# A Mamba/attention block with a mixture of experts on one core: narrower wide tiles, one sigmoid pass, and work moved among the stages

## The chip, the cores and the metric

The kernel runs on one core of a Trainium2 chip. It is one program of 28297 profiled instructions. The time is the device time of one execution in microseconds (us); "before" is the median of three timed executions. A separate execution was taken by the hardware profiler; all rows below come from it.

The engines run beside each other, each in the order in which its instructions were written out: PE (matrix products into PSUM[...]), DVE (vector work), ACT (activation functions, with a table that has to be loaded for some of them), POOL (vector work and scatters), and SP, which issues most DMAs. An instruction that waits holds up everything behind it on its engine.

## What is computed

All arithmetic is f32. The input x is 4 images of 256 channels by 32 x 32 positions (1024 positions per image). Cut to what matters here:

```
xn = norm(x) per position
for each of 4 channel groups: mamba           # project u and z, causal conv, SiLU, dt, a scan over
                                              # 1024 positions with 16 states x 128 channels
g  = sigmoid(conv(conv(x_concat)))            # the gates
xg = g * xm
R  = conv1x1(conv3(xg)) + xg
xm2 = conv1x1(conv3(concat(xs, R))) + xs      # the first half of conv3 is of the image itself: "own taps"
x_local = conv3(xm2);  x_global = attention(xm2), 8 heads
x_out = gelu(norm(concat(x_local, x_global) @ fc))
image = proj(norm(depthwise 3x3(norm(x_out)))) + x
# mixture of experts on the 4096 positions ("rows")
top 2 of 8 experts by gate logits, softmax weights
out = rows + sum over both experts of w * (gelu(row @ W1 + b1) @ W2 + b2)     # 256 -> 1024 -> 256
```

## The kernel before, in words

**The order is written out by hand.** Inside `tc.manual_schedule` (L1482) each engine executes in the order in which the Python code emits. The emission is a loop of ticks: `beat()` (L1441) advances every running generator, and each generator says with `yield n` in how many ticks it wants to go on. `start` adds generators, `one_by_one` chains them, `behind_flag` holds one back until a flag is set. `in_turn` (L411) makes items (usually products into PSUM) and uses each `lag` ticks later, one item every `every` ticks.

**The scan sets the ticks.** For each image, 4 channel groups n and 2 halves h are "parts"; a part has 16 steps (`scan`, L789). Each step emits on ACT the decay of three steps later (`decay`, `LEAD = 3`), on DVE one product into PSUM (`inflow`, L684) and one scan (`step`, L695), and on POOL one product (L703). `before`, `behind` and `group` (L739 to L755) say at which step of a part the preparations for the next one are emitted; `group[0]` holds the projections of z and u of the next channel group, the copies of z from PSUM, and SiLU, which loads its table, works on u and z, and loads back the table for Exp and Ln.

**Images overlap.** While image b is scanned, image b-1 goes through `convolutions` (parts 0 to 2), then `attention` in a pause of the scan after part 3, then `joined` (output projection and `fc`, norm, Gelu), in parts 4 and on. Image b-2 goes through `around` (3x3 taps) in the pause and `sent_off` (norm, projection, `experts.dispatch`) beside `joined`. `dispatch` finds for each row its place among the rows of its expert and scatters the rows to `XS` in DRAM, by 16 scatters on POOL per image. At the end of the scan, image 3 still has to go through all of this and image 2 through `around` and `sent_off`; the expert tiles are emitted between their pieces. A variable `pace` says every how many ticks a piece of a tile comes.

**Gates.** In `convolutions`, four products `gp` (two channel halves c, two position halves) are made; `sigmoid` reads them out of PSUM with ACT's Sigmoid, which needs its own table, and then loads the table for Exp and Ln again. This happens once for each c. POOL multiplies with the gates, then come ACT and DVE for the three taps. The generator `side` makes the products `fx` of the image's own taps and is advanced at every second tick of `gating`.

**Own taps.** For image 2 the own taps are computed earlier, in `normalised`, and kept in DRAM (`XD`); for the other images `convolutions` computes them first thing (`depthwise3` with `fdw_w`: one ACT and two DVE operations for each c).

**Expert tiles.** A tile is 256 rows of one expert. The tiles come in four series: two of 8 tiles that are full after images 1 and 2, the "rest" (19) and the "wide" ones (8) after image 3. A wide tile has 384 rows, so that an expert whose last tile would hold at most 128 rows needs none for them. Sixteen tiles of the first two series run, then 4 groups of one wide and 3 rest tiles. The last 7 rest tiles and the last 4 wide ones (`LATE`, `LATE_WIDE`) stand in a branch at the end and run only if a table has that many entries. For tile n+1, `ahead` emits during tile n the load of its rows (once the image's rows are sent), the load of its weights (2 MB), and `front` (transposes on PE, a copy to `xT` on DVE, four small DVE operations). `tile` then makes the hidden layer (`h`, L2174), Gelu on ACT, the second layer (`y`, L2186) by blocks of 128 rows, bias and weight on DVE, and one scatter with addition per block on POOL.

Of the kernel before, what the change touches and what calls it, by code (L numbers as in the profile page):

```python
# [9 lines left out]
F32 = mybir.dt.float32  # L10
# [38 lines left out]
LATE, LATE_WIDE = 7, 4  # L49
# [23 lines left out]
def network(  # L73
# [41 lines left out]
    XD = {b: dram.tile([P, NC2, N], F32, name=f"XD_{b}") for b in (2,) if b < B}  # L115
# [29 lines left out]
    with tc.tile_pool(name="w_conv", bufs=1) as wp, tc.tile_pool(  # L145
# [345 lines left out]
        def normalised(b):  # L491
# [30 lines left out]
            for c in range(NC2):  # L522
# [11 lines left out]
                if b in XD:  # L534
                    xd = a4(f"taps_{b}_{c}")
                    nc.scalar.activation(
                        xd, xl, AF.Identity, bias=col("fdw_b", c), scale=col("fdw_w", 3 * c + 1)
                    )
                    yield 1
                    for k, to, at in (  # L540
                        (0, slice(1, N), slice(0, N - 1)), (2, slice(0, N - 1), slice(1, N)),
                    ):
                        nc.vector.scalar_tensor_tensor(
                            xd[:, to], xl[:, at], col("fdw_w", 3 * c + k), xd[:, to],
                            ALU.mult, ALU.add,
                        )
                        yield 1
                    nc.sync.dma_start(XD[b][:, c, :], xd)

# [182 lines left out]
        def add_skip(b, n, h):  # L732
            c, rows = where(n)
            if n == 0 and h == 0:
# [16 lines left out]
                2: [(stack_x, 0)], 3: [(project_z, 0), (stack_x, 1)], 5: [(copy_z, 0)], 6: [(project_z, 1)],  # L751
                7: [(project_u, 0)], 8: [(copy_z, 1), (project_u, 1)], 12: [(silu,)],
# [94 lines left out]
        def convolutions(b):  # L847
# [41 lines left out]
            gs = []  # L889

            def sigmoid(c, gp):
                gs.append(a4(f"g_{b}_{c}"))
                for h in range(2):
                    nc.scalar.activation(  # L894
                        gs[c][:, half(h)], gp[h], AF.Sigmoid, bias=col("qpw_b", c)
                    )
                loaded[0] = None
                log_exp()

            def gating():  # L900
                yield from in_turn(range(NC2), gate, sigmoid)
# [29 lines left out]
            for n, ticks in enumerate(gating()):  # L931
                if n % 2 == 0:
                    next(side, None)
                yield ticks
# [20 lines left out]
            for _ in range(4):  # L955
# [197 lines left out]
        def inverse_deviation(name, xc, alone):  # L1153
# [9 lines left out]
            if alone:  # L1163
# [8 lines left out]
                yield 1  # L1172
            else:
# [12 lines left out]
        def joined(b):  # L1186
# [12 lines left out]
                ), every=2 if b == 0 else 1,  # L1199
            )  # L1200

            xc = XC[b] = a8(f"xc_{b}")
# [1136 lines left out]
```

## Time and profile before

| | us |
|---|---|
| timed executions: median (lowest to highest of 3) | 2253.38 (2250.92 to 2259.66) |
| the profiled execution's own time | 2258.26 |
| its span, first to last instruction | 2256.8 |
| busy in the span: PE, DVE, ACT, POOL | 1994.9, 1539.5, 1234.5, 1046.1 |
| scan's last step ends | about 1486 |
| attention of image 3 | about 1660 to 1746 |
| PE's last product of a tile | 2218.5 |

A row of a group reads: line, engine, operation, output<-inputs, shapes, count; then busy us and mean ns of one; then the idle time of the engine just before these instructions and what ended most of it. A row of a timeline reads: start, length, engine, line, operation, shapes, count and, in brackets, idle time before it and who ended it. A row of waits reads: who waited for whom, us in total, how many times, the longest. An f32 product shows as two records on PE. In the 40 slices of the page, PE is near full through the last third:

```
PE   6877878999978999987979999669999999999995
DVE  3989999768998978788898977984355265111111
```

### The profile page before, as it was taken

The page shows a single profiled execution, that of the slowest core. Times are in us where ns is not written, and L with a number is a line of the kernel's source. Part 1 is how long each engine was busy: PE and PEld are TensorE (multiplying, and loading weights), DVE is VectorE, ACT ScalarE, POOL GpSimd, SP SyncE. Part 2 cuts the span into 40 slices and gives each one's busy share as a digit, 9 for nine tenths or more (in the row PEclk, how much of TensorE's full clock was granted, in tenths as well). Part 3 has the DMA queues.
Part 4 walks back from the last instruction along what each step waited for, and adds up shares of the span by engine and source line. Part 5 has one row for each costly group of instructions (what it writes and reads, how often), then busy time and mean ns, then how long its engine had stood idle before and what let it go on. Part 6 is the DMA issues. An engine that isn't in the chain of part 4 may idle for free. (4 is left out here: it accounts for less than half of the span.)

```text
span 2256.8 us, 28297 instructions
## 1 busy us (share of the span) xinstructions
PE 1994.9 (88%) x8766; PEld 895.8 (40%) x8766; DVE 1539.5 (68%) x2211; ACT 1234.5 (55%) x2297; POOL 1046.1 (46%) x930
## 2 busy tenths in 40 slices
PE   6877878999978999987979999669999999999995
PEld 2112112322212332322223234125742677888884
DVE  3989999768998978788898977984355265111111
ACT  4665666678767676775756777325358422222221
POOL 0788878613877730675985035742040021422221
PEclk8898999999999999998899999779999999999997
DMA  3555553401453421243544013343240175866655
GB/s 99 140 155 125 123 136 76 118 10 56 119 131 86 99 48 38 71 113 84 157 98 100 20 37 91 80 154 95 92 118 1 45 216 164 257 186 180 168 160 161
DMA packets 156816, 248.79 MB, mean 110 GB/s; under 512 B 34597, under 2 KB 101701, under 8 KB 156521
## 3 DMA queue, kind: packets, MB, share of 16 engines
q1 hardware_dynamic: 136032, 220.59, 35.8%
q0 software_dynamic: 12976, 17.58, 4.0%
q10 hardware_dynamic: 7640, 8.65, 1.2%
q8 instruction: 73, 1.20, 0.2%
q14 instruction: 95, 0.77, 0.1%
HBM read 135.39 MB, written 35.84 MB: 76 GB/s over the span
## 5 line engine op out<-in xcount | busy, mean ns | idle before, releaser
L703 POOL TENSOR_TENSOR dA<-hs,cs 128x512 f32<-128x512 f32 x512 | 682.0, 1340 | 414.9 <-DVE hs L695 279.7
L674 ACT ACTIVATE dA<-dts,A 128x512 f32<-128x512 f32 x512 | 359.2, 718 | 190.8 <-DMA dts<-dt 105.7
L2206 POOL DMA_INDIRECT Y<-ys,dest x68 | 109.7, 1613 | 532.5 <-DVE ys L2200 525.7
L713 PE MATMUL yp<-dA,quads 128*32 128x512 f32 x1024 | 277.7, 638 | 71.9 <-POOL dA L703 60.9
L2179 ACT ACTIVATE hs<-h,b 128x256 f32<-128x256 f32 (+1 forms) x256 | 112.2, 485 | 384.2 <-PE h L2174 279.1
L1078 ACT ACTIVATE e<-st 128x512 f32<-128x512 f32 x512 | 264.0, 603 | 102.0 <-PE st L1068 84.3
L684 DVE TENSOR_TENSOR dBu<-dts,bs 128x512 f32<-128x512 f32 x384 | 260.3, 679 | 82.3 <-ACT g L894 14.0
L2174 PE MATMUL h<-xT,w 128*128 128x256 f32 (+1 forms) x1024 | 247.7, 398 | 13.5 <-DVE xT L2146 13.5
L2186 PE MATMUL y<-w,hs 128*128 128x256 f32 x1088 | 250.2, 382 | 5.0 <-ACT hs L2179 5.0
L695 DVE TENSOR_TENSOR_SCAN hs<-dA,last,dBu 128x512 f32<-128x512 f32 x192 | 243.9, 1270 | 3.5 <-POOL dt L624 1.7
L695 DVE TENSOR_TENSOR_SCAN hs<-dA,dBu 128x512 f32<-128x512 f32 x192 | 232.1, 1209 | 11.6 <-PE av L1088 3.9
L1124 DVE TENSOR_TENSOR e<-e,e 128x512 f32<-128x512 f32 x256 | 170.0, 727 | 83.8 <-ACT e L1078 45.8
L2174 PEld LDWEIGHTS h<-xT,w 128*128 128x128 f32 x1024 | 196.8, 193 | 64.8 <-DVE xT L2146 15.2
L2186 PEld LDWEIGHTS y<-w,hs 128*128 128x128 f32 x1088 | 205.8, 192 | 39.0 <-issue 6.1
L666 PE MATMUL bs<-u,xpwT_s 128*32 128x512 f32 x1024 | 161.3, 661 | 61.4 <-DVE hs L695 32.6
L2146 DVE COPY xT<-xp 128x512 f32<-128x512 f32 (+1 forms) x36 | 23.4, 660 | 268.1 <-PE xp L2143 242.7
L1068 PE MATMUL st<-qk 32*128 32x512 f32 x1024 | 175.9, 641 | 4.3 <-DVE ys L2195 2.7
L713 PEld LDWEIGHTS yp<-dA,quads 128*32 128x32 f32 x1024 | 49.8, 113 | 278.5 <-POOL dA L703 175.3
L1114 PE MATMUL av<-e,v 128*32 128x512 f32 x1024 | 139.9, 609 | 0.0
L1068 PEld LDWEIGHTS st<-qk 32*128 32x128 f32 x1024 | 60.0, 184 | 120.4 <-issue 87.5
L1088 PE MATMUL av<-e,every 128*32 128x512 f32 x512 | 87.7, 601 | 3.8 <-DVE e L1124 3.8
L666 PEld LDWEIGHTS bs<-u,xpwT_s 128*32 128x32 f32 x1024 | 25.1, 112 | 158.2 <-issue 58.1
(324 smaller groups left out, 2773.0 us busy)
## 6 DMA issues: line engine op xcount, KB each, us to landing
dts<-dt SPq DMA_DIRECT2D x512, 128.0 KB
w<-in_W_dram SPq DMA_DIRECT2D x124, 512.0 KB
cs<-cd SPq DMA_DIRECT2D x512, 64.0 KB
xd<-xn SPq DMA_DIRECT2D x64, 128.0 KB
xs<-XS SPq DMA_DIRECT2D x28, 260.0 KB
xn<-in_x_dram SPq DMA_DIRECT2D x8, 512.0 KB
XL<-xl SPq DMA_DIRECT2D x8, 512.0 KB
xl<-XL SPq DMA_DIRECT2D x4, 1024.0 KB
```

Source lines behind the costliest of these rows:

```text
L666: nc.tensor.matmul(bs[r], xpwT_s[:, n, s : s + 1].to_broadcast([P, 32]), T[b, n, "u"][:, half(h)], start=True, stop=True,)
L674: nc.scalar.activation(dA, T[b, n, h, "dts", g][:, 0, :], AF.Exp, scale=A[:, g, n, q : q + 1])
L684: nc.vector.tensor_tensor(dBu, T[b, n, h, "dts", g][:, 1, :], T[b, n, h, "bs", q], ALU.mult)
L695: nc.vector.tensor_tensor_scan(hs, T[b, n, h, "dA", i], dBu, 0.0 if h == 0 else last, ALU.mult, ALU.add)
L703: nc.gpsimd.tensor_tensor(dA, hs, T[b, n, h, "cs", q], ALU.mult)
L713: nc.tensor.matmul(T[b, n, h, "yp"][ts(g, 32)], quads, T[b, n, h, "dA", q * GD + g], start=False, stop=(q == GS - 1),)
L1068: nc.tensor.matmul(sts[i], k[r, ts(kt, P)], q[r, half(h)], start=True, stop=not shifted)
L1078: nc.scalar.activation(es[i], sts[i], AF.Exp, scale=1.0 / HD**0.5)
L1114: nc.tensor.matmul(accs[0][ts(i, HD)], v8[:, kt, ts(4 * g + i, HD)], es[i], start=(kt == 0), stop=(kt == NK - 1),)
L1124: nc.vector.tensor_tensor(first[i], first[i], es[i], ALU.add)
L2174: nc.tensor.matmul(hp[:, i, :], w1(c, k0 + i), xT[:, c, :], start=(c == 0), stop=(c == NC2 - 1))
L2186: nc.tensor.matmul(yp[:, ts(t % 2, C)], hidden(k)[:, ts(t, P)], w2(k), start=(k == 0), stop=(k == NHC - 1),)
```

## The change

- **Wide tiles of 320 rows** instead of 384 (`REST = 64`). Their third block has 64 rows. Its rows are loaded by a DMA of their own, its small DVE operations run apart, its second layer puts the products of even and odd k into the two halves of PSUM's partitions (`parts`), and ACT and DVE add the halves. The rest series has 21 entries, 9 of them late; 12 still run in the main stretch.
- **Gates**: `keep` copies `gp` out of PSUM with Identity and the bias; after the second c both are passed through Sigmoid in SBUF. For the last image the table for Exp and Ln isn't loaded right after, nor after the Gelu of its `joined`.
- **`side`** starts four ticks later and ends in the residual products.
- **Image 3's own taps** are computed by `taps_ahead` in the last pause, behind `local` and `around`, from `XL` into `XD`, and `convolutions` loads them.
- **`group[0]`**: second projection of z at step 4 (was 6), its copy at 7 (8), the projections of u at 8 and 10 (7 and 8), SiLU at 13 (12).
- **`joined` of image 2**: an item every second tick in both products, and `fc` waits until image 1's projection is emitted. **`inverse_deviation` of image 1** interleaves its two halves (8 ticks instead of 11).
- **`dispatch` of image 2** scatters at every second tick (each tick before).
- **`tiles`**: while a tile isn't ready, the generator looks again after 1 or 2 ticks instead of 4.

```diff
-LATE, LATE_WIDE = 7, 4
+LATE, LATE_WIDE = 9, 4
+REST = 64
...
-    XD = {b: dram.tile([P, NC2, N], F32, name=f"XD_{b}") for b in (2,) if b < B}
+    XD = {b: dram.tile([P, NC2, N], F32, name=f"XD_{b}") for b in (2, 3) if b < B}
...
+                if b in XD and b < B - 1:
+                    yield from own_taps(b, c, xl)
...
+        def taps_ahead(b):
+            for c in range(NC2):
+                xl = a4(f"xt_{b}_{c}")
+                nc.sync.dma_start(xl, XL[b][:, c, :])
+                yield 2
+                yield from own_taps(b, c, xl)
...
-                2: [(stack_x, 0)], 3: [(project_z, 0), (stack_x, 1)], 5: [(copy_z, 0)], 6: [(project_z, 1)],
-                7: [(project_u, 0)], 8: [(copy_z, 1), (project_u, 1)], 12: [(silu,)],
+                2: [(stack_x, 0)], 3: [(project_z, 0), (stack_x, 1)], 4: [(project_z, 1)],
+                5: [(copy_z, 0)], 7: [(copy_z, 1)], 8: [(project_u, 0)], 10: [(project_u, 1)], 13: [(silu,)],
...
-            def sigmoid(c, gp):
-                gs.append(a4(f"g_{b}_{c}"))
+            gs = [a4(f"g_{b}_{c}") for c in range(NC2)]
+            def keep(c, gp):
                 for h in range(2):
                     nc.scalar.activation(
-                        gs[c][:, half(h)], gp[h], AF.Sigmoid, bias=col("qpw_b", c)
+                        gs[c][:, half(h)], gp[h], AF.Identity, bias=col("qpw_b", c)
                     )
-                loaded[0] = None
-                log_exp()
+                if c == NC2 - 1:
+                    for g in gs:
+                        nc.scalar.activation(g, g, AF.Sigmoid)
+                    loaded[0] = None
+                    if beside:
+                        log_exp()
...
             for n, ticks in enumerate(gating()):
-                if n % 2 == 0:
+                if n >= 4 and n % 2 == 0:
                     next(side, None)
...
-            for _ in range(4):
+            for n in range(4):
+                if n % 2 == 0:
+                    next(side, None)
                 yield next(gated)
...
+            elif quick:
+                sq, var = [], []
+                for at in range(6):
+                    if at < 2:
+                        sq.append(squares(at))
+                    if 2 <= at < 4:
+                        var.append(column_mean(f"var_{name}_{at - 2}", sq[at - 2]))
+                    if 4 <= at:
+                        root(r[:, half(at - 4)], var[at - 4], eps5)
+                    yield 1
...
-                ), every=2 if b == 0 else 1,
+                ), every=2 if b in (0, B - 2) else 1,
             )
+            while b == B - 2 and not T.get(("projected", b - 1)):
+                yield 1
...
-                ), lag=(4, 4, 2, 2)[b], every=(4, 2, 1, 1)[b],
+                ), lag=(4, 4, 2, 2)[b], every=(4, 2, 2, 1)[b],
...
-            log_exp()
+            if b < B - 1:
+                log_exp()
...
-                    yield 4
+                    yield 2 if n in xs else 1 if n in got else 4
...
+                                *([taps_ahead(b)] if b == B - 1 and b in XD else []),
...
-    SERIES = (8, 8, 19, 8)
+    SERIES = (8, 8, 21, 8)
...
-                yield 2 if b == 0 or b == 1 and t % 2 else 1
+                yield 2 if b in (0, 2) or b == 1 and t % 2 else 1
...
-        return self.T + P if s == self.WIDE else self.T
+        return self.T + REST if s == self.WIDE else self.T
...
+            parts = P // n
             for k in range(NHC):
                 nc.tensor.matmul(
-                    yp[:, ts(t % 2, C)], hidden(k)[:, ts(t, P)], w2(k),
-                    start=(k == 0), stop=(k == NHC - 1),
+                    yp[ts(k % parts, n), ts(t % 2, C)], hidden(k)[:, ds(t * P, n)], w2(k),
+                    start=(k < parts), stop=(k >= NHC - parts),
                 )
...
+            if parts > 1:
+                other = m0.tile([REST, C], F32, tag="other", name=f"other_{j}", bufs=1)
+                nc.scalar.copy(other, yp[n:P, 0:C])
+                nc.vector.tensor_tensor(other, other, b2_s[0:n], ALU.add)
+                nc.vector.tensor_tensor(ys[0:n, t], yp[0:n, 0:C], other, ALU.add)
```

## The prediction

> **What bounds the kernel now.** I read the stretches first (busy microseconds by engine in each window), because the kernel has parts with different limits.
>
> ```profile
> core 0: us, PE busy (x) PEld busy (x) DVE busy (x) ACT busy (x) POOL busy (x), PEclk, DMA share, GB/s
> 55.50:300.60 245.10, 192.40 (x668) 44.78 (x668) 234.66 (x271) 148.58 (x281) 200.74 (x165) 0.91 0.56 136
> ...
> 1200.00:1318.00 118.00, 116.58 (x710) 33.61 (x710) 95.97 (x126) 85.51 (x165) 21.92 (x19) 1.00 0.16 42
> 1318.00:1486.00 168.00, 135.36 (x466) 43.62 (x465) 147.09 (x215) 90.75 (x172) 106.50 (x102) 0.87 0.35 95
> 1486.00:1660.00 174.00, 150.56 (x596) 100.66 (x596) 79.01 (x160) 63.01 (x99) 35.85 (x45) 0.95 0.38 112
> ...
> 1919.00:2218.50 299.50, 299.08 (x1362) 251.10 (x1362) 51.66 (x165) 68.85 (x152) 81.88 (x89) 1.00 0.65 179
> ```
>
> Until 1486 us the state scan runs and DVE sets the pace: 235 of 245 us busy in the first full stretch, a step being one scan and one product, about 1.7 us. The three attention pauses in it (1200:1318 is the last) are PE's. From 1486 on PE does the rest, and from 1919 to 2218 it is never idle, so there only PE work counts. Of the 174 us after the scan PE works 151. The waits of PE there, in total and longest:
>
> ```profile
> PE h L2174 <- DVE xT L2146: 10.5, 1, 10.5
> PE y L2186 <- ACT hs L2179: 4.4, 1, 4.4
> PE xp L2143 <- DMA xs<-XS: 1.5, 1, 1.5
> PE gp L884 <- ACT qs L877: 1.5, 1, 1.5
> ...
> PE op L730 <- POOL xl L365: 1.0, 1, 1.0
> ```
>
> These 19 us lie between 1490 and 1533, and PE is the bound from there until the last tile: each one filled with tile work ends the kernel so much earlier. After PE's last matmul of a tile (2218.5) come 38 us of adding rows, reading back and writing out, which nothing here touches.
>
> **Part by part.**
>
> *Tiles of 320 rows.* The rows of PE for one wide tile (start, length; a row ends in effect where the next starts):
>
> ```profile
> 1962.44 10.48 PE L2174 MATMUL h<-xT,w 128*128 128x384 f32 x32
> 1972.76 3.62 PE L2186 MATMUL y<-w,hs 128*128 128x256 f32 x16
> ...
> 1976.65 7.07 PE L2186 MATMUL y<-w,hs 128*128 128x256 f32 x32
> 1983.56 7.07 PE L2174 MATMUL h<-xT,w 128*128 128x256 f32 x32
> ```
>
> The first layer takes 10.32 us for 32 records of 384 columns (322 ns each); the next tile takes 6.91 for 32 of 256 (216). So 64 columns are worth 53 ns, and 320 columns save 32 x 53 = 1.7 us. The third block's second layer is 16 records of 216 ns, 3.45 us. With 64 rows it has as many records, but the even and the odd ones go to different halves of the array's columns. Whether halves overlap I read from the row that already uses column groups, four of them:
>
> ```profile
> 1497.04 2.78 PE L870 MATMUL qd<-xm,qdwT_s 128*32 128x512 f32 x24
> ```
>
> 24 records of 512 columns one after another would take 24 x 0.43 = 10.3 us; they take 2.78, four at a time. So I let two at a time take half: 1.7 us saved. Against it speaks the Trainium skill, "TensorEngine Tiling (Array Packing)", Key Properties: changing the tiling mode drains the engine, and this block changes it twice in each tile. The trace has the price:
>
> ```profile
> 1367.87 1.02 PE L608 MATMUL dtp<-u,wdt 128*128 128x512 f32 x2
> 1368.82 1.06 PE L666 MATMUL bs<-u,xpwT_s 128*32 128x512 f32 x8
> 1369.70 1.04 PE L713 MATMUL yp<-dA,quads 128*32 128x512 f32 x8
> 1370.70 1.55 PE L406 MATMUL var_lgn<-sq_lgn,ones_mean 128*128 128x512 f32 x3
> ```
>
> Two full records need 0.86 and the narrow ones start after 0.95; eight narrow ones need 0.86 and the full ones start after 1.00. A change costs about 0.1, so the rule takes 0.2 back per tile. The half-size transposes give 0.2 (6 records took 0.66). Sum 3.4 per tile, **13.8 us** for four. Were the halves served in turn, it would be about 7; that is the lower end. The added ACT copy and two DVE additions (0.6 and up to 0.7 each by the rows of like size), the split row load and the four extra small DVE operations are covered by ACT and DVE that are busy 69 and 52 of 299 us; uncovered they would cost 2 us per tile. Running the reference's routing on its inputs gives 1024, 1065, 1023, 1012, 1006, 1048, 1041, 973 rows per expert: three exceed a multiple of 256 by 1 to 64, so the same 32 tiles run, four wide, and no late one.
>
> *After the scan.* Image 3's own taps (2 ACT operations of 1.24, 4 DVE of 1.28 us) leave the head of the stretch; tile 0's front is asked for every tick or second tick instead of every fourth; the sigmoids cost one table load, not two pairs. Today tile 0's xT copy stands on DVE at 1509.6 behind four of those taps (5.1 us) and ten of `around`'s (11.6 us), though its rows landed at 1495. Image 1's last rows are sent three ticks earlier by the quick variance (some 5 us), so xT should be there by about 1492. PE gets 10 us of tile work for the 10.5 us hole. The 4.4 us hole is ACT's:
>
> ```profile
> 1522.58 1.28 ACT L894 ACT_TABLE_LOAD   x1
> 1523.88 1.27 ACT L894 ACTIVATE g<-gp,V 128x512 f32<-128x512 f32 x2
> 1525.16 1.28 ACT L381 ACT_TABLE_LOAD   x1
> 1526.45 1.28 ACT L894 ACT_TABLE_LOAD   x1
> ...
> 1530.32 1.28 ACT L2179 ACT_TABLE_LOAD   x1
> ```
>
> Nine microseconds until the tile's next Gelu become 4 copies (2.5), two sigmoids (2.1) and 2 loads (2.6), the copies apart from the rest: 4.7 in one piece. I count 15 of the 19 us; what remains is the landing of the rows and the wait of `op`. Ends: 6 (image 3's chain is late for its products and PE waits there) and 19. What is late next is PE itself. **15 us**.
>
> *Image 2's row scatters at every second tick.* 16 scatters go through POOL and its queue in front of attention; at its start DVE's ys addition is late and PE waits 2.7 us (page: st, 4.3 idle, 2.7 by ys). Attention has over 30 ticks for 32, POOL is idle there (12 of 86 us), and their first reader is tile 8, after it. **2 us**, ends 0 and 2.7.
>
> *Image 2's join slowed, image 1's variance quick.* After the third pause two images' chains issue products at once. DVE's waits there:
>
> ```profile
> DVE hs L695 <- issue: 3.5, 1, 3.5
> DVE dBu L684 <- PE bs L666: 3.1, 1, 3.1
> DVE dBu L684 <- ACT xm L736: 2.6, 1, 2.6
> DVE dBu L684 <- ACT xglo L1197: 2.3, 2, 1.7
> ```
>
> With three smaller ones (1.1, 1.0, 1.0) they make 14.6 us. Half the products per tick and the second chain waiting for the first removes what PE's crowding causes; the Gelu and its loads (5 us of ACT) come later in the scan and may cost a step. I take two thirds, **10 us**, ends 0 and 14.6. The wait for image 1's projection ends some 18 ticks in, the join some 40, of 64: nothing after the scan waits for it.
>
> *Gates beside the scan (three images).* DVE waits 14.0 us in six places for ACT's g, which holds PSUM banks through a table load. The copies free them; fx products leave the crowded ticks. But ACT's block does not shrink much: 7.7 us become 2.4 + 1.28 + 2.1 + 1.28 = 7.1, now 4.7 in one piece, and SiLU (1.28 + 1.27 + 1.05 + 1.28 = 4.9) comes a step nearer. `decay` is three steps, 5.1 us, ahead. Here the Trainium skill, "ScalarE: Activation LUTs", What ACT_TABLE_LOAD costs, differs: 2.66 us per switch with its drain; the rows show 1.28 and the next activation 0.01 to 0.02 later. By the page two switches fewer save 5.3 us of ACT per image, by the row 2.6, which the two extra passes (2.1) nearly use up. I go by the row: **5 us** of the 14, ends -3 and 13.
>
> *z, u and SiLU moved.* DVE waited 4.6 us in all for z; SiLU one step later leaves three steps to `project_dt`. Zero, ends -5 and +4.6.
>
> *Image 3's taps in the pause.* DVE works 96 of 118 us there, PE bounds it; 5.1 us of DVE, 2.5 of ACT, two loads and two stores on SP's queue (DMA share 0.16) fit, the last tap perhaps after it. SP's stores wait for DVE, and the first spread loads behind them are ten steps away. Zero; uncovered 5.
>
> Sum: 13.8 + 15 + 2 + 10 + 5 = 45.8 us. The profiled execution took 2258.26 us (span 2256.8 and 1.5 around it), 4.9 above the median 2253.38. From it 2212.5; from the median **2208 us**.
>
> **Rivals.** (1) *The scan gives nothing*: the freed waits come back as ACT waits of the decays, since ACT's work there is nearly unchanged. For it: the 4.7 and 4.9 us blocks against 5.1 us of lead; against: the PE waits of the join are not ACT's. 30.8 saved, 2223. (2) *The hole moves*: PE starts tile 0 early, then waits for image 3's gates; 5 of 15 saved, 2218. Against it: some 20 us of tile pieces precede the first products. (3) *Halves in turn*: 2214. (4) *Everything goes*: join 14.6, gates 13: 2195. (5) *Slower, by late tiles*: one expert too many with a small rest, or over 12 tiles left, and the closing branch runs all 13 late tiles, 9 x 14.3 + 4 x 17.3 = 198 us, 2406. It decides with the first tile over; by the row counts four wide places and twelve others are exactly filled, and one row moved to the next expert changes neither. (6) *No change*.
>
> **How the numbers follow.** Forecast 0.38; (1) 0.22, (2) 0.14, (3) 0.08, (4) 0.12, (5) 0.02, (6) 0.03, 0.01 for another loss. The forecast's own terms vary by about 9 us either way (2199 to 2217); (1) with (2) reaches 2230, (4) with a bit more 2191: the range is 2191 to 2230. A measurement tells 0.5% (11 us) from no change; all but the last three cases are faster by more: 0.94, 0.03, 0.03.
>
> **What would show it.** The h row of a wide tile at 8.6 us, its third block at about 1.75 for 16 records; no PE wait for xT over 3 us after the scan; PE from the scan's end to attention some 15 us shorter; the stretch after the third pause some 10 us shorter; four loads at the sigmoid line instead of eight. Wrong if DVE's waits on dA grow where those on g fall, if PE waits for rp's or gp's inputs between 1490 and 1550, or if a late tile appears.

## The result, and the profile after

The changed kernel takes 2218.06 us (median of 6, 2211.61 to 2225.49) against 2254.15 us for the kernel before (median of 6). The ratio is 0.9839, with an interval of 0.9819 to 0.9858. So 36 us are saved where 45.8 were forecast. In a later comparison it took 2213.3 us against 2253.12, ratio 0.9841 (0.9816 to 0.9866). The direction and the range held, and the forecast itself was 10 us too low (5 against the second measurement).

The profiled execution of the changed kernel took 2211.61 us, the shortest of its six. That of the kernel before took 2258.26, above the median. Between the spans of the two profiles (2256.8 and 2209.9) lie 46.9 us, almost the sum of the forecast. The difference between 46.9 and 36 needs an explanation of its own, which is given below.

Busy microseconds by engine in stretches of the changed kernel's scan (the first full image, the third pause, the rest):

```profile
core 0: us, PE busy (x) PEld busy (x) DVE busy (x) ACT busy (x) POOL busy (x), PEclk, DMA share, GB/s
56.10:298.10 242.00, 193.76 (x668) 44.64 (x668) 234.16 (x272) 148.97 (x281) 200.35 (x165) 0.90 0.57 139
1181.00:1297.00 116.00, 113.81 (x694) 32.73 (x690) 95.85 (x125) 83.32 (x159) 18.64 (x15) 1.00 0.16 40
1296.10:1464.30 168.20, 135.53 (x465) 41.21 (x464) 145.98 (x215) 92.34 (x175) 108.41 (x105) 0.88 0.38 104
```

The picture of limits is the old one: DVE paces the scan, PE the rest. The scan ends at 1464.3 instead of 1485.1, which is 20.8 us earlier. From there to PE's last product of a tile it is one PE-bound stretch. I compare it with the same stretch of the kernel before, first before, then after:

```profile
1485.10:2218.30 733.20, 701.25 (x3269) 501.75 (x3268) 263.21 (x640) 260.08 (x497) 160.81 (x186) 0.98 0.48 136
```

```profile
1464.30:2170.40 706.10, 683.52 (x3269) 490.67 (x3270) 262.27 (x656) 257.74 (x500) 159.85 (x182) 0.99 0.50 143
```

The stretch is 27.1 us shorter: PE is busy for 17.7 us less (701.25 to 683.52), and its holes shrink by 9.4 us (31.95 to 22.58, each as stretch less busy time). The end after the last product stayed within 1 us of its 38.5.

The same stretch in four stages (up to attention, attention, from there to the 14th tile, and from the 14th tile to the last), first before, then after:

```profile
1485.20:1655.50 170.30, 148.92 (x587) 99.98 (x586) 79.22 (x160) 62.46 (x97) 34.70 (x44) 0.95 0.37 109
1655.50:1747.30 91.80, 89.11 (x641) 25.09 (x640) 51.40 (x79) 69.63 (x137) 14.15 (x20) 0.98 0.12 34
1747.30:1919.30 172.00, 164.19 (x685) 125.62 (x684) 81.26 (x238) 59.15 (x111) 29.98 (x34) 0.97 0.49 141
1919.30:2218.30 299.00, 298.94 (x1362) 251.06 (x1362) 51.23 (x164) 68.85 (x152) 81.88 (x89) 1.00 0.65 179
```

```profile
1464.30:1625.00 160.70, 148.56 (x588) 101.24 (x592) 73.46 (x148) 57.74 (x94) 25.39 (x24) 0.94 0.40 122
1625.00:1711.00 86.00, 86.00 (x640) 24.29 (x632) 53.27 (x89) 69.51 (x137) 23.13 (x35) 1.00 0.15 45
1711.00:1881.70 170.70, 160.26 (x686) 122.10 (x685) 81.05 (x238) 61.86 (x113) 30.93 (x36) 1.00 0.50 143
1881.70:2170.50 288.80, 288.80 (x1362) 243.10 (x1362) 54.50 (x184) 68.63 (x156) 80.39 (x87) 1.00 0.67 184
```

From first product to first product, the stages became shorter by 10.0, 5.4, 1.4 and 10.2 us.

The rows of PE around one wide tile (start, length, shapes, count):

```profile
1920.66 1.16 PE L2194 MATMUL xp<-ident,xs 128*128 128x128 f32 x6
1921.74 3.72 PE L2248 MATMUL y<-w,hs 128*128 128x256 f32 x16
1925.30 8.78 PE L2235 MATMUL h<-xT,w 128*128 128x320 f32 x32
1933.92 3.62 PE L2248 MATMUL y<-w,hs 128*128 128x256 f32 x16
...
1937.81 5.50 PE L2248 MATMUL y<-w,hs 128*128 128x256 f32 x32
1943.23 7.17 PE L2235 MATMUL h<-xT,w 128*128 128x256 f32 x32
```

The first layer takes 8.62 us from start to start (8.6 forecast). The last 32 records of the second layer take 5.42 us from start to start; the 16 full ones among them are worth 3.45, which leaves 1.97 for the third block (1.75 forecast). From the start of its first layer to the start of the next tile's, a wide tile takes 17.93 instead of 21.12 us.

PE's waits from the scan's end on, in total and longest:

```profile
PE xp L2194 <- DMA xs<-XS: 7.2, 1, 7.2
PE rp L399 <- DVE d L433: 4.6, 1, 4.6
PE h L2235 <- DVE xT L2198: 4.0, 2, 2.2
PE y L2248 <- ACT hs L2240: 2.5, 3, 1.7
PE var_fin L409 <- ACT sq_fin L1180: 2.5, 1, 2.5
```

The 10.5 us wait for xT and the 4.4 us wait for hs are gone, as forecast. New are 7.2 us for the rows of tile 0, one step earlier in the same chain, and 4.6 us for image 3's d. The sigmoids show what was forecast too. Up to the tile's next Gelu two loads stand where five stood, and the block takes 7.05 us instead of 9.03:

```profile
1490.99 2.42 ACT L908 ACTIVATE g<-gp,V 128x512 f32<-128x512 f32 x4 [3.53 <-PE gp L899]
1493.43 1.28 ACT L913 ACT_TABLE_LOAD   x1
1494.72 2.00 ACT L913 ACTIVATE g<-g 128x1024 f32<-128x1024 f32 x2
1496.74 1.28 ACT L2240 ACT_TABLE_LOAD   x1
```

DVE's waits between the third pause and the scan's end:

```profile
DVE dBu L699 <- ACT XR L1768: 4.1, 2, 3.2
DVE xi L1213 <- ACT r_fin L391: 3.9, 1, 3.9
DVE hs L710 <- PE av L1108: 3.9, 1, 3.9
DVE gate L1817 <- PE gate L1807: 2.4, 1, 2.4
```

These four make 14.3 us. Before the change the waits that the prediction named made 14.6, and three of them are gone (issue, bs and xm, 9.2 us). Those for xglo stand at 2.7 us in two smaller rows, and r_fin and av, 1.0 and 1.3 us before, have grown to 3.9 each. That part of the scan (parts 4 to 7 of the last image) took 168.4 us after and 168.6 before, where 10 us less were forecast. From the scan's end to attention it is 160.3 us instead of 170.3, where 15 less were forecast.

### The profile page after: what moved, and what is told of

Read it like the earlier page. It is cut to its first block, busy times and chain, and to the rows that moved or that the text cites. A ratio compares the mean times of both kernels' runs of the same rounds, so it can differ in the third digit from the quotient of the medians.

```text
span 2209.9 us, 28348 instructions
## 1 busy us (share of the span) xinstructions
PE 1971.1 (89%) x8766; PEld 881.5 (40%) x8766; DVE 1532.8 (69%) x2231; ACT 1230.8 (56%) x2302; POOL 1047.0 (47%) x930
## 5 line engine op out<-in xcount | busy, mean ns | idle before, releaser
L728 PE MATMUL yp<-dA,quads 128*32 128x512 f32 x1024 | 261.6, 639 | 62.2 <-POOL dA L718 49.3
L2248 PE MATMUL y<-w,hs 128*128 128x256 f32 (+1 forms) x1088 | 243.6, 382 | 2.5 <-ACT hs L2240 2.5
L2235 PE MATMUL h<-xT,w 128*128 128x256 f32 (+1 forms) x1024 | 238.3, 389 | 4.0 <-DVE xT L2198 4.0
L710 DVE TENSOR_TENSOR_SCAN hs<-dA,dBu 128x512 f32<-128x512 f32 x192 | 232.0, 1209 | 10.2 <-PE av L1108 5.1
L2248 PEld LDWEIGHTS y<-w,hs 128*128 128x128 f32 (+1 forms) x1088 | 197.0, 188 | 39.4 <-issue 8.9
L699 DVE TENSOR_TENSOR bs<-dts,bs 128x512 f32<-128x512 f32 x128 | 86.2, 674 | 2.1 <-DMA dts<-dt 2.1
```

The source lines that it names most:

```text
L699: nc.vector.tensor_tensor(dBu, T[b, n, h, "dts", g][:, 1, :], T[b, n, h, "bs", q], ALU.mult)
L710: nc.vector.tensor_tensor_scan(hs, T[b, n, h, "dA", i], dBu, 0.0 if h == 0 else last, ALU.mult, ALU.add)
L728: nc.tensor.matmul(T[b, n, h, "yp"][ts(g, 32)], quads, T[b, n, h, "dA", q * GD + g], start=False, stop=(q == GS - 1),)
L2235: nc.tensor.matmul(hp[:, i, :], w1(c, k0 + i), xT[:, c, :], start=(c == 0), stop=(c == NC2 - 1))
L2248: nc.tensor.matmul(yp[ts(k % parts, n), ts(t % 2, C)], hidden(k)[:, ds(t * P, n)], w2(k), start=(k < parts), stop=(k >= NHC - parts),)
```

## The experiments

The twelve kernels ran in three sets of four, each set on another chip. All edits are made to the changed kernel. "The stretch" is from the scan's end to PE's last tile product, 706.1 us in the changed kernel. "The nine parts" are parts 0 to 2 of images 1 to 3, in which the gates stand: 333.5 us in the changed kernel, 343.8 before.

### First set: one part undone at a time

**Wide tiles of 384 rows again.**

```diff
-LATE, LATE_WIDE = 9, 4
-REST = 64
+LATE, LATE_WIDE = 7, 4
+REST = 128
-    SERIES = (8, 8, 21, 8)
+    SERIES = (8, 8, 19, 8)
```

> The changed kernel with its wide tiles back at 384 rows (19 rest tiles, 7 of them late); all else as changed. Theory (halves of the columns overlap, 3.3 us per wide tile, of which some 0.5 us is given back where the 64-row transposes stand): the stretch from the 14th tile to the last product of a tile grows from 288.8 to about 299 us, a wide tile from 18.0 to 21.3, and the time by 10 us over the changed kernel. Rival (the gain is elsewhere and the wide tiles are worth only their first layer): 7 us. If the tiles hide under DMA: no change.

Measured: 2244.61 us, ratio to before 0.9932 (0.9908 to 0.9956). A wide tile is at 21.12 us again, and the stretch from the 14th tile to the last at 301.0 instead of 288.8 us. But 2.0 of these 12.2 us belong to other things. In this execution PE was granted half its clock for 3.4 us in the first of these tiles, whose first layer took 8.70 us from start to start (7.01 in the changed kernel), and the second of these tiles began some 0.3 us late:

```profile
1905.22 8.86 PE L2235 MATMUL h<-xT,w 128*128 128x256 f32 x32 [2.00 <-DVE xT L2198]
```

The kernel before, which has no half clock in this stretch, takes 299.0 us. So the four wide tiles are worth 10.2 us, not 13.8. The rows of one tile say the same: a wide tile itself saves 3.19 us; 0.42 goes back in front of it, where the six transposes, now with a 64-row block among them, take 1.08 us from start to start (six full ones took 0.66); and the rows behind the transposes and behind the third block take some 0.1 us more each. That leaves about 2.57 us, or 10.3 for four.

**Join of image 2 and variance of image 1 as before.**

```diff
-                ), every=2 if b in (0, B - 2) else 1,
+                ), every=2 if b == 0 else 1,
-            while b == B - 2 and not T.get(("projected", b - 1)):
-                yield 1
...
-                ), lag=(4, 4, 2, 2)[b], every=(4, 2, 2, 1)[b],
+                ), lag=(4, 4, 2, 2)[b], every=(4, 2, 1, 1)[b],
...
-            yield from inverse_deviation(f"fin_{b}", xc, b == B - 1, b == 1)
+            yield from inverse_deviation(f"fin_{b}", xc, b == B - 1)
```

> The changed kernel with image 2's join and image 1's variance as before (an item every tick, no wait for the projection, variance by halves). Theory of the forecast: the stretch of the scan after the third pause (168.3 us in the changed kernel) grows by about 10. Rival, from the changed kernel's trace: the spacing moved DVE's waits (3.9 us on r_fin, 4.1 on XR, 2.4 on the gate logits took the place of the old ones), so the stretch stays within 3 us, and the time too.

Measured: 2231.44 us, ratio 0.9874 (0.984 to 0.9907). Parts 4 to 7 of the last image take 172.0 us. In the other runs whose code there is that of the changed kernel they take 164.2 to 169.9. So undoing it costs some 2 to 8 us in this one profile; the longest of DVE's waits there is 7.6 us for ACT's u, whose projections and SiLU the changed kernel emits later. Against the kernel before, at 168.6, this part of the scan gained nothing in the first profile and up to 4 us in others.

**z, u and SiLU at their old steps.**

```diff
-                2: [(stack_x, 0)], 3: [(project_z, 0), (stack_x, 1)], 4: [(project_z, 1)],
-                5: [(copy_z, 0)], 7: [(copy_z, 1)], 8: [(project_u, 0)], 10: [(project_u, 1)], 13: [(silu,)],
+                2: [(stack_x, 0)], 3: [(project_z, 0), (stack_x, 1)], 5: [(copy_z, 0)], 6: [(project_z, 1)],
+                7: [(project_u, 0)], 8: [(copy_z, 1), (project_u, 1)], 12: [(silu,)],
```

> The changed kernel with the projections of z and u, the copy of z and SiLU at their old steps. Theory of the forecast: nothing, 0 within 5 us. Rival, from the trace: the scan's parts outside the gates became shorter by some 11 us in all (the parts after the pause of image 2 by 3.5 and 2.0, image 0's third by 2.5), and undoing this alone gives most of it back: 8 to 11 us longer until the scan's end, with DVE's waits for the copies of z and for xglo back.

Measured: 2236.79 us, ratio 0.991 (0.9884 to 0.9936). The nine parts take 334.1 us. Parts 4 to 7 of images 1 and 2 take 295.4 instead of 287.2, those of the last image 162.3 instead of 168.4. In this profile, what the move wins in the one place it gives back in the other.

**Sigmoids from PSUM and the own-taps products early, for images 0 to 2.**

```diff
-                        gs[c][:, half(h)], gp[h], AF.Identity, bias=col("qpw_b", c)
+                        gs[c][:, half(h)], gp[h], AF.Sigmoid if beside else AF.Identity, bias=col("qpw_b", c)
-                if c == NC2 - 1:
+                if beside:
+                    loaded[0] = None
+                    log_exp()
+                elif c == NC2 - 1:
...
-                if n >= 4 and n % 2 == 0:
+                if n % 2 == 0:
...
-                if n % 2 == 0:
-                    next(side, None)
```

> The changed kernel with images 0 to 2 passed through Sigmoid straight from PSUM, once for each c, and the products of the side at their old ticks; image 3's gates as changed. Theory of the forecast: 5 us longer in parts 0 and 1 of images 1 to 3 (DVE's waits for g, 14 us, come back; the 4.0 us waits of DVE's taps for ACT's taps, one in each part 1, go). Rival: 10 us, since part 2 became shorter by 4.2 us as well and only the side can have done it; or 0, if the waits only changed their names.

Measured: 2248.6 us, ratio 0.9943 (0.9921 to 0.9965). The nine parts take 353.7 us, 20 more than in the changed kernel and 10 more than before. DVE's wait for the gates in part 0 of image 3 shows a part of it:

```profile
DVE dBu L699 <- ACT g L908: 10.8, 2, 7.9
DVE hs L710 <- POOL dt L639: 2.4, 1, 2.4
```

In the changed kernel the first of these is 4.6 us, in the kernel before 4.2.

**A stall in attention in all four.** The totals of this set don't fit their stretches: the first three lose 13 to 27 us against the changed kernel where their edits explain at most half. The rest is attention of image 3. From the last tile before it to the first tile after it, it took 86.4 us in the changed kernel and 101.5, 96.7, 101.5 and 101.9 us in these four, whose code is the same there. ACT's rows in the run of the old order of z, u and SiLU:

```profile
1635.32 4.13 ACT L1098 ACTIVATE e<-st 128x512 f32<-128x512 f32 x8 [0.23 <-PE st L1088]
1642.96 2.06 ACT L1098 ACTIVATE e<-st 128x512 f32<-128x512 f32 x4 [3.50 <-PE st L1088]
1648.00 0.60 ACT L1098 ACTIVATE e<-st 128x512 f32<-128x512 f32 x1 [2.98 <-PE av L1134]
...
1658.02 4.03 ACT L1098 ACTIVATE e<-st 128x512 f32<-128x512 f32 x8 [6.57 <-remote]
```

ACT's exponentials wait 3.5, 3.0 and 6.6 us, though by PE's rows (whose ends are modelled) the logits for the first were finished in time. DVE stands for 9.63 us as well, and PE is granted half its clock in two windows of 6.8 us that start within and at the end of the stall. The stall begins some 10 us into attention and is over 28 us into it; in that time POOL sends image 2's rows, one scatter every 1.27 us. The next sets ask whether it belongs to the code or to the chip on which this set ran.

### Second set: the changed kernel beside three variants

> The changed kernel as it is, timed beside the three that follow. In its first profile the attention of image 3 took 86.4 us with the clock full, in the four variants 96.7 to 101.9 with stalls and a halved clock, though their code there is the same. If the stall belongs to the place where tile and scatter code fall in those variants, attention takes 86 to 87 us again and the time is 2212 to 2222. If it comes by chance or from the chip, attention takes 92 to 102 us here too, and the time is 2222 to 2235; the differences to the four variants then shrink by up to 15 us.

Measured: 2213.3 us, ratio 0.9841. Attention takes 86.4 us, and the stretch 706.2.

**Image 2's scatters at attention's pace.**

```diff
                 es = ahead
+                experts.beside = es[3]
...
             for t in range(NT):
+                if b == self.B - 2:
+                    nc.gpsimd.tensor_copy(apart, self.beside[:, 0:1])
                 nc.gpsimd.memset(apart, 0.0)
```

> Each of image 2's 16 row scatters on POOL first copies one column of the exponentials that attention has just made, so that they come at attention's pace (5.2 us apart) and not one right behind another (1.27 us). If scatters in close order hold up the signals between PE, ACT and DVE in attention, its stretch is 86 to 88 us whatever the chip, and no PE wait over 0.5 us is left in it. If the stalls have another cause, they stay where they are in the changed kernel of the same call. If only the small extra waits count, attention is up to 2 us longer than its 86.4.

Measured: 2214.11 us, ratio 0.9843 (0.9814 to 0.9872). From the fourth on, the scatters come 5.2 us apart, and attention takes 86.6 us. But the changed kernel beside it had no stall either, so this run tells nothing about the scatters as a cause. It shows only that spacing them costs nothing.

**Tile 0's front at every third tick.**

```diff
-                    yield 2 if n in xs else 1 if n in got else 4
+                    yield (2 if n else 3) if n in xs else 1 if n in got else 4
```

> Tile 0's front is asked for every third tick instead of every second, so that PE's last scan sums stand before its transposes. My theory of the missing 5 us after the scan is that the sums, and with them image 3's y, op and qd, stand behind transposes that wait 7.2 us for their rows: then ACT's y starts some 2 us after the scan's end instead of 8.2, DVE's d and PE's rp come earlier (the 4.6 us wait for d at 1510 falls below 1), and the stretch from the scan's end to attention is 156 us instead of 160.4. The rival is that PE has too little tile work there, and the 7.2 us wait is only spent elsewhere: the stretch stays within 1.5 us of 160.4, or it is longer because the tile's front is later.

Measured: 2215.78 us, ratio 0.9834 (0.9808 to 0.9859), which the changed kernel's 2213.3 doesn't differ from. In the changed kernel PE does this at the scan's end (1464.3):

```profile
1469.38 1.08 PE L2194 MATMUL xp<-ident,xs 128*128 128x128 f32 x4 [7.19 <-DMA xs<-XS]
1470.39 1.94 PE L728 MATMUL yp<-dA,quads 128*32 128x512 f32 x8
```

The transposes of tile 0 stand first and wait for their rows, and the last sums of the scan, from which image 3's chain begins, stand behind them. In the variant the sums come first. ACT's first y follows 5.6 us after the scan's end instead of 8.1 (I expected 2), and attention begins 155.7 us after it instead of 160.3 (156 expected). The wait for d falls from 4.6 to 0.7 us. But these waits stand in the variant from there on:

```profile
PE h L2235 <- DVE xT L2198: 7.3, 3, 3.3
PE var_fin L409 <- ACT sq_fin L1180: 4.6, 1, 4.6
PE places L1843 <- DVE ex L1838: 3.3, 1, 3.3
```

In the changed kernel they were 4.0, 2.5 and 1.0. The whole stretch is 704.5 us, and four kernels with the changed kernel's code there took 703.7 to 706.2, so nothing is left that can be told. Even the 4.6 us up to attention are not shown to come from the edit: the next run keeps both waits (7.2 and 4.6 us) and begins attention after 156.5 us, with 10.2 us of half clock in that time where the changed kernel has 20.5 (the variant, too, has 10.2). So the theory of what delays the start of image 3's chain holds, since the waits go when the order is turned; that removing them saves their length does not.

**The 64-row block in one half of PSUM.**

```diff
-            parts = P // n
+            parts = 1
...
-            if parts > 1:
+            if False:
...
-                    ys[:, t0 : t + 1], yp[:, 0 : some * C].rearrange("p (t c) -> p t c", t=some),
+                    ys[0:n, t0 : t + 1], yp[0:n, 0 : some * C].rearrange("p (t c) -> p t c", t=some),
```

> The 64-row block of a wide tile multiplies even and odd k one after another in one half of PSUM's partitions, without ACT's copy. If the two halves of the array work beside each other, the third block's second layer goes from about 1.75 us to 3.45, a wide tile from 18.0 to 19.7, and the stretch of the tiles after attention is 6 to 7 us longer. If they are served in turn already, nothing changes on PE. If changing the tiling mode had a price of its own, the loss is smaller by it.

Measured: 2219.94 us, ratio 0.9877 (0.9843 to 0.9912). The row that answers to the 5.50 us of the changed kernel:

```profile
1935.29 7.22 PE L2248 MATMUL y<-w,hs 128*128 128x256 f32 x32
```

So 16 records in two halves side by side take 1.97 us, and in one half 3.7 us (7.15 from start to start, less 3.45). A wide tile takes 19.65 us, 1.72 more, and the stretch from the 14th tile 295.6 us, 6.8 more. The halves do work beside each other. Against 16 full records' 3.45 us, and half of it, either form loses some 0.25 us.

### Third set

**The old steps of z, u and SiLU once more**, with no edit but the one shown above.

> The same kernel as in the run of the old order of z, u and SiLU. There attention took 101.5 us with stalls and a halved clock. If those belong to this kernel, it takes about 100 us again and the time is 2232 to 2240. If they came with the chip of that call, attention takes 86 to 87 us and the time is 2213 to 2222, which makes the move of z, u and SiLU worth 0 to 4 us. The parts 0 to 2 of images 1 to 3 together should again take 334 us, as in the changed kernel (333.5).

Measured: 2220.71 us, ratio 0.986 (0.9834 to 0.9887), where the same kernel gave 0.991 in the first set. Attention in the first set and here:

```profile
1630.00:1731.40 101.40, 96.24 (x640) 27.02 (x640) 53.82 (x90) 69.60 (x137) 21.39 (x35) 0.93 0.12 38
```

```profile
1632.10:1718.50 86.40, 86.40 (x642) 24.54 (x641) 53.57 (x90) 69.53 (x137) 23.12 (x35) 1.00 0.15 45
```

All four timed executions of the first set (2234.5 to 2244.7 us) lie above all four here (2215.9 to 2225.2). So the 15 us belong to that chip or that set and not to one execution or to this edit, and the four totals of the first set are too high by 10 to 15 us. The kernel before was timed in the first set too, and there it took 2257.11 us, only 3 to 6 more than in the others. So the stall may need the changed kernel as well. One thing that all four variants share with it and not with the kernel before is that the 16 scatters of image 2 all fall into attention, some 1.3 us apart, where before eight of them started ahead of it. The changed kernel itself never ran on that chip. There this variant was 20 us ahead of the kernel before, here it is 30.

The nine parts take 335.9 us and the stretch 706.2, as in the changed kernel. Parts 4 to 7 take 291.2 us in images 1 and 2 and 163.5 in the last, where six profiles of the changed code gave 287.1 to 290.7 and 164.2 to 169.9. So the move of z, u and SiLU is worth nothing that can be measured.

**Sigmoids from PSUM alone**; the own-taps products keep their later start.

```diff
-                        gs[c][:, half(h)], gp[h], AF.Identity, bias=col("qpw_b", c)
+                        gs[c][:, half(h)], gp[h], AF.Sigmoid if beside else AF.Identity, bias=col("qpw_b", c)
-                if c == NC2 - 1:
+                if beside:
+                    loaded[0] = None
+                    log_exp()
+                elif c == NC2 - 1:
```

> For images 0 to 2 the sigmoids read PSUM again, with the table loaded and loaded back for each c; the later start of the own-taps products stays. Undoing both together brought the nine parts (0 to 2 of images 1 to 3) from 333.5 to 353.8 us, with DVE's waits for g at 6.2, 6.3 and 10.8. If the copies that free PSUM do it, these parts are at 345 to 354 here too and the scan ends some 12 to 20 us later. If the fewer products in the crowded ticks do it, they are at 334 to 340.

Measured: 2220.43 us, ratio 0.9867 (0.9842 to 0.9891). The nine parts take 345.6 us, which lies in the range that I had named for the copies (345 to 354); both edits undone gave 353.7. Two things lie in this number. The parts 0 and 1, in which the gates and the own-taps products stand, take 237.2 us together: the changed code 232.4 to 235.0, both edits undone 247.0. So in these parts the copies are worth some 2 to 5 us, and the later own-taps products some 10, beside the new places of z, u and SiLU. All three parts 2 took 36.1 instead of 32.9 us, 9.6 together, each with 6.8 us of half clock. Part 2 has such windows in some executions of the changed code too, but in 10 of 27 parts of nine profiles; with the sigmoids from PSUM it had them in all six parts of two profiles. Whether the old gates bring them on or chance did stays open, and with it whether the copies are worth 2 us or more than 10.

**Only image 1's variance as before.**

```diff
-            yield from inverse_deviation(f"fin_{b}", xc, b == B - 1, b == 1)
+            yield from inverse_deviation(f"fin_{b}", xc, b == B - 1)
```

> Only image 1's variance before its projection is as before, with its halves one after another, 11 ticks instead of 8. If the quick form is what puts DVE's new wait of 3.9 us for ACT's r into part 4 of the last image, that wait goes and parts 4 to 7 take 164 to 166 us instead of 168.3. If it earned its place, by rows that are sent three ticks earlier, the wait for tile 0's rows after the scan grows from 7.2 to 10 to 12 us and the stretch from the scan's end to attention from 160.4 to 163 to 166. If neither, both stretches stay within 1.5 us.

Measured: 2214.79 us, ratio 0.9837 (0.9815 to 0.9858). The stretch is 706.5 us. The first case holds in its wait: that of 3.9 us for r_fin is gone, and parts 4 to 7 of the last image take 162.8 us (the changed code 164.2 to 169.9). The second doesn't: the wait for tile 0's rows doesn't grow, it falls to 1.8 us: the rows land some 11.5 us after the scan's end instead of 5, but tile 0's front now stands behind the scan's last sums. Attention begins 154.5 us after the scan's end instead of 160.3, and the 6 us are given back before the last tile. The quick variance does send the rows earlier, and it is worth nothing.

**Image 3's own taps at the head of the last stretch again.**

```diff
-    XD = {b: dram.tile([P, NC2, N], F32, name=f"XD_{b}") for b in (2, 3) if b < B}
+    XD = {b: dram.tile([P, NC2, N], F32, name=f"XD_{b}") for b in (2,) if b < B}
```

> Only image 3's own taps are back at the head of the last stretch. I counted them as hidden in the pause and part of the 15 us after the scan. If so, the third pause is 2 us shorter here (122.7 instead of 124.8), and the stretch from the scan's end to attention 5 to 8 us longer, since DVE's 5.1 us stand again before image 3's gates. The rival is that DVE has room there: that stretch grows by less than 2 us, and moving the taps won nothing.

Measured: 2218.48 us, ratio 0.9832 (0.98 to 0.9865). The third pause is 1.5 us shorter (123.3) and the stretch 2.8 us longer (708.9). Tile and attention order shift here (six tiles before attention instead of five), so only the whole stretch can be compared. That leaves 1.3 us, less than the 2.7 us by which four kernels with the changed kernel's code differ in pause and stretch together. So the rival, that DVE has room there anyway, fits, and my 5 to 8 us do not.

## Why the prediction came out right, and which of its steps failed

The direction and the range held. The sum came out right in part by luck: the terms for the wide tiles, for the part after the scan and for the join were too high by some 17 us together, and parts of the scan to which the forecast gave nothing made up for them.

| term | forecast, us | in the two profiles, us |
|---|---|---|
| wide tiles | 13.8 | 10.2 |
| after the scan | 15 | 10.0 up to attention, 1.4 behind it |
| image 2's scatters | 2 | 5.4 in attention, 2.7 of them the wait that was named |
| join | 10 | 0.2 |
| gates and own-taps products | 5 | 10.3 in the nine parts |
| z, u, SiLU, image 3's own taps, all else in the scan | 0 | 10.3 |
| end after the last product | 0 | -1.0 |

**Wide tiles.** The 322 and 216 ns per record gave the first layer to 0.02 us, and the reading of the four-group row, that groups of columns work beside each other, was right: in one half of PSUM a tile takes 1.72 us more. The drain for a changed tiling mode, of which the Trainium skill's "TensorEngine Tiling (Array Packing)", Key Properties, warns, stayed small, as the rows of 0.1 us had said: 1.97 us for the third block where 1.72, half of 3.45, would be ideal, and 0.1 us in the row behind it. The step that failed is the front: the 0.2 us that half-size transposes were to save became a loss of 0.42.

**After the scan.** The step that failed is "PE gets 10 us of tile work for the 10.5 us hole". The rows were on time: tile 0's first layer starts 8 us after the scan's end, where I had put xT at 7. But PE had the transposes in its queue ahead of the scan's last sums and stood at them for 7.2 us, and image 3's chain with it; then came 4.6 us of waiting for d, the input of rp. PE waiting for rp's input between 1490 and 1550 was one of the prediction's own signs of being wrong. The second rival, that the hole moves, was right in that the hole moved, though to another place than it gave. Up to attention PE's holes shrank by 9.3 us, not by 15; behind attention they grew by 2.6.

**Scatters.** The 2.7 us wait for ys is gone. The other 2.7 us were in no term of mine: before, 3.4 us of attention ran at half clock, by my estimate a loss of half of that, and the last 1 us stays open. In the whole stretch PE was at half clock and busy for 23.4 us before and 13.8 after; half of the difference, 4.8 us, is my estimate of what the clock gave there.

**Join.** The step that failed is "I take two thirds" of the waits. Three of the waits named went, and longer ones for r_fin, av, XR and the gate logits stand in their place. I take it that the work moved out of the crowded ticks was only put into the next ones; no run shows that by itself. Undone, it costs 2 to 8 us in one profile, but against the kernel before it gains nothing that shows.

**Gates and own-taps products.** In nine profiles of the changed code the nine parts take 331 to 340 us, so the 10.3 us are 4 to 13 against one profile of before. I had put the saving on the copies that free PSUM. The runs give 8 to 10 us to `side`, which I mentioned in half a sentence, and to the copies 2 us or, with part 2 counted, 12; this stays open. With the old gates and the old `side`, the later places of z and u came with 10 us more (353.7 against 343.8, one profile each); with the new ones they cost nothing.

**What no term named.** Of the 10.3 us, 8.1 lie in parts 4 to 7 of images 1 and 2 (295.3 to 287.2 us; 287.1 to 290.7 in six profiles of the changed code) and 3.3 in the first parts of image 0 (93.4 to 90.1; 89.8 to 93.1), less 1.1 elsewhere. No run isolates their cause. In the two profiles with the old places of z, u and SiLU, the first of these is 295.4 and 291.2. For image 0 the profile of the changed kernel is a short one.

**From 46.9 to 36 us.** The first rival (the scan gives nothing) is refuted: over six profiles with exactly the changed kernel's code in the scan it ends between 1464.0 and 1471.7 us, against 1485.1 before. But the 20.8 us come from an execution at the short end of this range. What the medians lack is in the profiled executions: that of before was 4.1 us above its median, that of after 6.4 below, together 10.5. I had subtracted all the waits found in a long execution from a shorter median, and some of those waits may be what made it long. Two window rows of the same part of the scan, in the changed kernel and in the run with the later front, whose code is the same there, show the size of such differences:

```profile
734.60:767.50 32.90, 29.94 (x105) 10.71 (x106) 30.27 (x36) 22.05 (x46) 26.22 (x20) 1.00 0.47 108
```

```profile
737.90:774.00 36.10, 33.10 (x105) 11.16 (x106) 30.28 (x35) 22.07 (x46) 26.26 (x20) 0.91 0.41 99
```

The same 105 matmuls take 3.2 us longer at a granted clock of 0.91, and DVE's work is as long as before, so it waits (4.8 us for PE's bs instead of 1.6). That such windows also make the 14 us between the shortest and the longest timed run is likely, but no profile of a long one was taken.

No variant beat the changed kernel by more than the measurement can tell.

## What to carry to other kernels

A hole that is closed by asking earlier for its work can come back one instruction earlier: before asking earlier, look up what will stand behind the new instruction in its queue. Here, putting that in front took the waits away and still saved no time that could be measured, so a wait is not yet a saving. Where waits come from crowding, a list of waits is no sum of savings: new waits of the same size can stand in the next ticks, so compare the length of the stretch and not the names. Before subtracting waits from a median, see whether the profiled execution is a long one of its kind, and compare equal parts of two profiles with the granted clock beside them: one window of half clock turned 10.2 us for the wide tiles into 12.2.

## What the hardware showed that was not expected

- **Half clock comes in windows of about 3.4 us, and most cost about 1.6 us where PE is near the path.** In each of the fourteen profiles, the stretches of half clock last 3.4, 6.8, 10.2 us and so on, all but one of them. Of the 27 parts 2 of images 1 to 3 in nine profiles of the same code, the 17 without half clock take 32.9 us and the six with 6.8 us of it 36.1; of the four with 3.4 us three take 34.5 and one 32.9.
- **The same kernel stalled in attention in one set and not in another**, 101.4 against 86.4 us. Four kernels of one chip had it, nine profiles of the changed kernel and its variants on other chips did not. During the stall ACT and DVE waited for work that PE's rows, with their modelled ends, show as done. Whether the chip alone or the scatters beside it cause this stays open; the run that spaced the scatters came when there was no stall to remove.
- **Two halves of the array's columns nearly double the rate of products with 64 columns:** 1.97 us for 16 records against 3.7 one after another.
